# Four convolution and attention layers on one core: statistics gathered after 22 parts, weights and shifts of layer 0's end moved

## The chip, the cores and the metric

The kernel runs on 1 of the 8 cores of a Trainium2 chip. Its metric is the device time of one execution in microseconds (us), lower is better. Names used below: PE is TensorE (matrix products, with PEld its weight loads), DVE is VectorE, ACT is ScalarE, POOL is GpSimd, SP is SyncE, which mostly issues DMAs. Each engine works through its own list of instructions in order and waits for other engines through semaphores.

## The reference, cut to what matters

The input is x of 16 images, 256 channels, 28 x 28. Four layers follow each other.

```python
# layer 0
out = sign(x)                                   # binary activation, forward value
y = conv3x3(out, sign(weights)) * mean(|weights|)
x = (y - mean(y)) * rsqrt(var(y) + EPS) * gamma + beta + x      # mean, var over images and places
# layer 1
residual = prelu(x); z = sign(x + a_move)
y = prelu(bn(conv3x3(z, a_w)));  y = gate(.5*x + .5*y) * y * residual
y = bn(y) + residual;  u = prelu(bn(conv1x1(sign(y + f_move), f_w)))
x = bn(gate(.5*y + .5*u) * u) + y
# layer 2
out = prelu(conv3x3(sign(batchnorm(x)), sf1*sign(w1)))
out = prelu(conv3x3(sign(batchnorm(out)), sf2*sign(w2)))
x = prelu(batchnorm(out) + x)                   # batchnorm: statistics over images and places
# layer 3
q, k, v = Wq x, Wk x, Wv x
x = Wp (softmax(q k^T / 8) v) + x
```

Every batch norm needs the mean and the variance of a whole convolution's output before the next layer can read its first value. The convolutions of layers 0 and 2 therefore end in a point where everything waits for the last statistic.

## The kernel before

The 256 channels lie as two groups of 128 partitions. Layers 0 and 2 use the same function, `sign_layer`: a 3 x 3 convolution of signs by signs. Two groups of output channels are packed into one product (weights `a + 4095 b`), so one 128-wide product gives both, and they are taken apart afterwards. `sign_layer` walks through blocks. In layer 0 a block is a whole image (784 places), except that the last image is cut into a half and two quarters (`PARTS`, 33 parts in all; a whole image counts as two). In layer 2 a block is half an image (392 places, `HALVES`, 32 parts). For block j it emits, in this order:

1. `products(j)`: 18 products of PE for each half (6 packed weight chunks of 3 taps), into a PSUM tile `cv` of which there are three;
2. `sign_image`: on ACT, the signs of the next image, into one of two padded buffers `fpads`;
3. `post(j - 1)`: DVE's work on the block before. In layer 0 (`post0`) that is four or two BN_STATS over the block's values `n`, and a POOL-issued DMA of a finished image's int16 values to DRAM (`n0d`). In layer 2 (`post2`) it is a prelu into `p`, BN_STATS, twice, and on ACT a `square` of the sums, whose total is a guard against inexact results (`doubts`);
4. once, `moments.gather()`, at the first block whose part number is above `EARLY` (26): it merges the first 26 parts' statistics into three numbers, with one BN_AGGR per channel group and a scaling;
5. in layer 0, one entry of `steps`: pieces of weight work for later layers (load, ACT part, DVE part), dealt out one for each half image;
6. `apart(j)`: on ACT two passes that round the packed product (`t`, then `ab` or `n`), on DVE one that takes the other half (`ab` or `n`).

In this part the order on PE, ACT, DVE and SP is the program's own order (`manual_schedule`). POOL's order isn't; it is set by the framework's scheduler.

At the end of the convolution `Moments.__call__` merges the gathered numbers with the late parts' (a BN_AGGR over `fin`, 3 + 6 numbers for each late part), and `norm` or `sign_norm` works out scale and shift in a chain of tiny DVE instructions with one ACT square root. `keep_busy` gives PE dummy products (`unused`) for that time.

From layer 0 to layer 1: `norm("l0", ...)` gives the scale `r`, then calls `first`, which emits `enter(0, 0)` (image 0, channel group 0: scaled `n` plus x, one DVE instruction over two SBUF tensors). Then DVE works out `c = mean * r` and `bi0 = beta - c` in `norm`, and `zb1 = bi0 + a_move` behind it. `sign1(0, 0)` on ACT uses `zb1` as its bias; `transform` on DVE and `widen` make operands for PE's first product of layer 1. The values `n` are read back from `n0d` by SP DMAs, two buffers of which are there. Layer 1 is a loop over images (`iteration`), in which DVE and ACT prepare image b + 1 while PE works on image b.

The last two weight steps of layer 0 before the gates' weights are the sixth chunk of layer 2's first weights (`sign_weights`: ACT `sg`, DVE `wpk`) and the split of layer 1's 1 x 1 weights (`fw_step`, `split2`: DVE clips `stf`, ACT copies `fw`, DVE takes the remainder). Their loads are called by the steps two places earlier (`load_ahead`).

Of the kernel before, what the change touches and what calls it, by code (L numbers as in the profile page):

```python
# [51 lines left out]
IMAGES = [(i, 0, S) for i in range(B - 1)]  # L52
EARLY = 26
MC = 112
# [29 lines left out]
def forward(ctx: ExitStack, tc: tile.TileContext, d: dict, out: bass.AP, careful: bool):  # L84
# [16 lines left out]
    def pv(name):  # L101
        return vec[:, VECS.index(name), :]
# [27 lines left out]
    def vtile(name):  # L130
        return const.tile([P, 2], F32, name=name)

    def tt(o, a, b, op):
        V.tensor_tensor(o, a, b, op)  # L134
        return o
# [50 lines left out]

    def norm(name, moments, gamma, beta, sf=None, then=lambda r: None):


        half, e = vtile(name + "_half"), vtile(name + "_e")  # L190
        V.tensor_scalar(half, gamma, -0.5, None, ALU.mult)
        if sf is not None:

            tt(e, sf, sf, ALU.mult)
            V.tensor_scalar(e, e, 1e-30, 1.0 / EPS, ALU.max, ALU.mult)
            V.reciprocal(e, e)
        m, var = moments()
        v, c = vtile(name + "_v"), vtile(name + "_c")
        if sf is not None:
            tt(v, var, e, ALU.add)  # L200
        else:
            V.tensor_scalar(v, var, EPS, None, ALU.add)
        r = rsqrt(name, v, half)
        then(r)
        tt(c, m, r, ALU.mult)
        return r, tt(c, beta, c, ALU.subtract)

# [114 lines left out]
    def sign_layer(pads, w, temp, room, sign, post, steps, moments, blocks, together=1):  # L322
# [44 lines left out]
        with tc.manual_schedule(engines={ET.PE, ET.Activation, ET.DVE, ET.SP}):  # L367
            sign_image(0)
            for j, block in enumerate(blocks):
# [4 lines left out]
                if block[1] == 0 and block[0] + 1 < B:  # L374
                    sign_image(block[0] + 1)
                if j > 0:
                    post(blocks[j - 1], abs_[j - 1])
                if first_part(block) > EARLY and not gathered:
                    gathered = True
                    moments.gather()  # L380
                for p in range(len(pieces(block))):
# [3 lines left out]
                    late = step() if step else None  # L385
                apart(j)
            post(blocks[-1], abs_[-1])
        assert not steps and not late
# [31 lines left out]
    with tc.tile_pool(name="ps_conv", bufs=3, space=PSUM) as psc, \  # L420
# [13 lines left out]
        with tc.tile_pool(name="ph1", bufs=1) as ph:  # L434
# [109 lines left out]
            for t in (w_1, w_2):  # L544
                nc.gpsimd.memset(t, 0.0)

            def constants():
                for p in pads:
                    nc.gpsimd.memset(p, 0.0)
# [43 lines left out]
            for (_, high, low), taps, add_up, sign in zip(w1_steps, ahead[0::3], ahead[1::3], ahead[2::3]):  # L593
                steps += [taps, lambda high=high, low=low: (high(), low)[1], add_up, sign]
            steps += [ahead[-1], gate_weights]
            for i in (21, 17, 13, 9):
                steps[i:i] = [None]

            def post0(block, ab):
                b, r0, rows = block  # L600
                for mo in range(2):
                    for h, _, m in pieces(block):
                        V.bn_stats(mom.part(first_part(block) + h, mo), ab[:, mo, h * HN:h * HN + m * S])
                if r0 + rows == S:
                    nc.gpsimd.dma_start(out=n0d[b], in_=ns[b])

            mom = block_moments("l0", PARTS)
# [268 lines left out]
            def iteration(b):  # L876
# [67 lines left out]
                if two:  # L944
                    branch2(b - 2, 1, g[:, 1])
                    for k in range(2):
                        squares2(b - 2, k)
                lates = [s.work() for s in aside[b][::-1]]
                for s in aside[b + 1]:
                    s.load()  # L950
# [27 lines left out]

            with tc.manual_schedule(engines={ET.PE, ET.DVE, ET.Activation}):
                sc0, bi0 = norm("l0", mom, pv("g0"), pv("b0"), sf0, first)  # L980
                mom.doubt(doubts[:, 0:2 * NB])
                zb1 = tt(vtile("zb1"), bi0, pv("a_move"), ALU.add)
                sign1(0, 0)
# [95 lines left out]
        with tc.tile_pool(name="ph2", bufs=1) as ph:  # L1079
# [36 lines left out]
            def post2(order, alpha, mom, doubt):  # L1116
# [4 lines left out]
                def post(block, ab):  # L1121
# [18 lines left out]

                    for h, _, m in pieces(block) if not careful else ():

                        if i < B - 1:
                            square(h, m)
                        else:
                            last_squares.append(lambda h=h, m=m: square(h, m))
                return post
# [621 lines left out]
```

## Time and profile before

| | us |
|---|---|
| median of 3 runs | 970.87 (970.1 to 971.01) |
| the profiled execution | 969.59 |
| its span, first to last instruction | 967.7 |
| layer 0, from the start to PE's last product | 0 to 107.5 |
| between layers 0 and 1 (to PE's first product) | 107.5 to 117.7 |
| layer 1 and its end | 117.7 to 473.1 |
| layer 2, first convolution, then the gap | 473.1 to 571.2, to 579.1 |
| layer 2, second convolution, then the gap | 579.1 to 677.2, to about 690 |
| layer 3 | to 967.7 |

In the profile's timeline each line is a start, a duration, the engine, the line of the kernel, the operation, output <- inputs with their shapes, and in brackets how long the engine had stood idle and what ended that. `x2` after a shape means two instructions merged into one line. The granted clock is the share of TensorE's full clock that the throttle let through. `keep_busy` products count as busy PE time though they compute nothing, so PE's busy share between the layers says nothing of useful work.

### The profile page before, as it was taken

The page shows a single profiled execution, that of the slowest core. Times are in us where ns is not written, and L with a number is a line of the kernel's source. Part 1 is how long each engine was busy: PE and PEld are TensorE (multiplying, and loading weights), DVE is VectorE, ACT ScalarE, POOL GpSimd, SP SyncE. Part 2 cuts the span into 40 slices and gives each one's busy share as a digit, 9 for nine tenths or more (in the row PEclk, how much of TensorE's full clock was granted, in tenths as well). Part 3 has the DMA queues.
Part 4 walks back from the last instruction along what each step waited for, and adds up shares of the span by engine and source line. Part 5 has one row for each costly group of instructions (what it writes and reads, how often), then busy time and mean ns, then how long its engine had stood idle before and what let it go on. Part 6 is the DMA issues. An engine that isn't in the chain of part 4 may idle for free.

```text
span 967.7 us, 14795 instructions
## 1 busy us (share of the span) xinstructions
PE 942.3 (97%) x5609; PEld 582.1 (60%) x5615; DVE 773.8 (80%) x1418; ACT 721.7 (75%) x1198; POOL 140.9 (15%) x149
## 2 busy tenths in 40 slices
PE   7999899999999999999999999999999999999995
PEld 3555478788788778876555555555444444444442
DVE  4776878899998899976799987999756867777765
ACT  6887667888888888864888868887666667676652
POOL 3001100000000000000100000000145343444431
PEclk9999999999999999999999999999999999999999
DMA  9978512344433233100680000000043343435212
GB/s 348 343 267 304 177 34 84 116 149 146 145 125 100 100 113 111 60 34 34 232 334 1 1 1 1 2 1 1 5 76 88 80 122 72 129 71 131 67 67 104
DMA packets 26948, 105.82 MB, mean 109 GB/s; under 512 B 3490, under 2 KB 7268, under 8 KB 26868
## 3 DMA queue, kind: packets, MB, share of 16 engines
q1 hardware_dynamic: 20948, 73.44, 21.4%
q0 software_dynamic: 5632, 30.54, 11.7%
q8 instruction: 46, 0.75, 0.3%
q10 hardware_dynamic: 288, 0.80, 0.2%
q14 instruction: 34, 0.28, 0.1%
HBM read 72.67 MB, written 32.11 MB: 108 GB/s over the span
## 4 chain that ended last, share of the span: by engine, by line
PE 46%; DVE 3%; ACT 1%; issue 1%; DVEq 0%; ACTq 0%
PE cv L340 19%; PE sc L1344 8%; PE av L1365 8%; PE mi L1321 4%; PE sm L1407 2%; PE mi L1425 2%; PE sm L1365 1%; DVE p L1131 1%; DVE ab L354 0%; ACT es L1348 0%; DVE l2b_fin L1133 0%; DVE l2c_fin L1133 0%; DVE r L1391 0%; DVE p L1308 0%; DVE p L1307 0%
## 5 line engine op out<-in xcount | busy, mean ns | idle before, releaser
L340 PE MATMUL cv<-fpads,wpk 128*128 128x392 f16 (+1 forms) x1746 | 294.7, 331 | 4.3 <-DVE wpk L267 2.3
L718 PE MATMUL cv<-vs,w 128*128 128x392 bf16 (+1 forms) x1536 | 286.9, 356 | 4.1 <-DVE vs L134 4.1
L340 PEld LDWEIGHTS <-wpk 128*128 128x128 f16 x1746 | 169.0, 97 | 130.4 <-DVE wpk L267 3.7
L718 PEld LDWEIGHTS cv<-vs,w 128*128 128x128 f32 x768 | 142.5, 190 | 11.0 <-ACT vs L700 0.2
L1348 ACT ACTIVATE es<-sc 128x784 f32<-128x784 f32 x112 | 87.3, 822 | 41.1 <-PE sc L1344 41.1
L718 PEld LDWEIGHTS <-w 128*128 128x128 f16 x768 | 67.9, 101 | 59.6 <-issue 18.7
L1344 PE MATMUL sc<-q,keyswa 64*128 64x392 f32 x448 | 89.9, 513 | 0.9 <-ACT es L1348 0.9
L1131 DVE SCALAR_TENSOR_TENSOR p<-ab,vec 128x392 f32<-128x392 f32 x128 | 79.1, 618 | 2.3
L1365 PE MATMUL av<-es,v 128*64 128x392 f32 x448 | 80.7, 499 | 0.0
L1358 POOL TENSOR_TENSOR sum<-sum,es 128x784 f32<-128x784 f32 x32 | 67.2, 2099 | 3.1 <-ACT es L1348 0.6
L1344 PEld LDWEIGHTS sc<-q,keyswa 64*128 64x128 f32 x448 | 38.9, 186 | 44.0 <-issue 17.1
L351 ACT ACTIVATE t<-cv,rounding 128x392 f32<-128x392 f32 (+2 forms) x82 | 51.8, 632 | 13.3 <-PE cv L340 10.4
L861 POOL DMA_DIRECT2D x2d<-x x16 | 8.6, 537 | 343.4 <-DVE x L855 280.9
L1332 DVE COPY keyswa<-mi 64x392 f32<-64x392 f32 x31 | 16.3, 565 | 52.6 <-ACT q L1328 52.6
L1365 PEld LDWEIGHTS av<-es,v 128*64 128x64 f32 x448 | 29.4, 136 | 47.4 <-issue 47.0
L700 ACT CAST vs<-vs 128x840 fp32r<-128x840 bf16 x63 | 54.1, 882 | 2.2 <-DVE vs L134 2.2
L1136 ACT ACTIVATE t<-ab 128x392 f32<-128x392 f32 x64 | 33.5, 524 | 27.9 <-DVE ab L354 27.9
L833 PE MATMUL cv<-z,fw 128*128 128x392 f32 x256 | 48.9, 342 | 1.0 <-ACT z L825 0.8
L354 DVE SCALAR_TENSOR_TENSOR ab<-ab,cv 128x392 f32<-128x392 f32 x64 | 35.5, 555 | 17.5 <-ACT ab L352 17.5
L833 PEld LDWEIGHTS cv<-z,fw 128*128 128x128 f32 x256 | 45.7, 188 | 2.3 <-ACT z L825 2.1
L1321 PE MATMUL mi<-p,wqk 128*128 128x392 f32 x124 | 45.3, 506 | 0.3 <-DVE p L1308 0.3
L1356 POOL TENSOR_TENSOR sum<-es 128x784 f32<-128x784 f32 x16 | 30.0, 1877 | 91.0 <-ACT es L1348 91.0
(288 smaller groups left out, 1519.8 us busy)
## 6 DMA issues: line engine op xcount, KB each, us to landing
xs<-in_x_dram SPq DMA_DIRECT2D x30, 784.0 KB, 5.5
x2d<-x POOLq DMA_DIRECT2D x16, 784.0 KB, 3.8
out_dram<-p SPq DMA_DIRECT2D x15, 784.0 KB, 3.9
p<-x2d POOLq DMA_DIRECT2D x14, 784.0 KB, 6.9
p<-x2d SPq DMA_DIRECT2D x13, 784.0 KB, 15.6
n0d<-n POOLq DMA_DIRECT2D x16, 392.0 KB, 5.1
n<-n0d SPq DMA_DIRECT2D x16, 392.0 KB, 3.1
st<-in_w_dram SPq DMA_DIRECT2D x12, 384.0 KB, 6.7
```

The source lines that it names most:

```text
L340: T.matmul(pss[j][:, n // size if careful else h, :rows * S].rearrange("p (a b) -> p a b", b=S), lhsT=w[:, n, t, :], rhs=pads[:, blocks[j] ...
L351: A.activation(by_halves(t, blocks[j]), ps, AF.Identity, bias=rounding, scale=1.0 / PACK)
L354: V.scalar_tensor_tensor(a, b, -PACK, ps, ALU.mult, ALU.add)
L700: copy(v, w)
L718: T.matmul(ps.rearrange("p (a b) -> p a b", b=S), lhsT=w[:, k, c, u, mo * P:(mo + 1) * P], rhs=v[:, b % 2, u, k, :, c:c + S], start=((part ...
L833: T.matmul(ps[:, h, :HN], lhsT=w[:, k, mo * P:(mo + 1) * P], rhs=z2[b][:, k, h * HN:(h + 1) * HN], start=(k + i == 0), stop=(k + i == 2),)
L1131: V.scalar_tensor_tensor(p, y, alpha[:, mo:mo + 1], y, ALU.mult, ALU.max)
L1321: T.matmul(ps[:, h, :HN], lhsT=wqk[:, k, :], rhs=x[b][:, k, h * HN:(h + 1) * HN], start=(k == 0), stop=(k == 1))
L1344: T.matmul(ps[:, h, :HN], lhsT=chunk[rows], rhs=qs[b][rows], start=True, stop=True)
L1348: A.activation(e, ps[:, :, :HN], AF.Exp, scale=0.125)
L1358: (V if late else nc.gpsimd).tensor_tensor(sums[b, late], sums[b, late], e, ALU.add)
L1365: T.matmul(ps[64 * h:64 * h + 64, :HN], lhsT=w, rhs=e[:, h, :], start=start, stop=stop)
```

## The change

Four things change.

- `EARLY` is 22 and not 26: in all three convolutions of `sign_layer` the gather merges 22 parts and comes four parts earlier, and four more parts stay for the final BN_AGGR.
- In layer 2 `post` returns its squares instead of emitting them, and `sign_layer` emits them after `apart(j)`. On ACT the order goes from signs, square, t, ab to signs, t, ab, square. The last image's squares are still emitted after the convolution.
- The last two weight steps are taken out of layer 0's list (two empty places stand for them) and are emitted in iteration 0 of layer 1, behind the second channel group's sums and `widen`.
- In layer 0's norm `c`, `zb1` and `bi0` are computed on POOL, `zb1` from a sum `moved = b0 + a_move` that DVE makes early in layer 0. `enter(0, 1)` now follows `enter(0, 0)` on DVE at once.

```diff
-EARLY = 26
+EARLY = 22
...
-    def norm(name, moments, gamma, beta, sf=None, then=lambda r: None):
+    def norm(name, moments, gamma, beta, sf=None, then=lambda r: None, shifts=()):
...
         then(r)
-        tt(c, m, r, ALU.mult)
-        return r, tt(c, beta, c, ALU.subtract)
+        if not shifts:
+            tt(c, m, r, ALU.mult)
+            return r, tt(c, beta, c, ALU.subtract)
+        cs = [vtile(f"{name}_c{i}") for i in range(len(shifts))]
+        nc.gpsimd.tensor_tensor(c, m, r, ALU.mult)
+        for o, b in zip(cs, shifts):
+            nc.gpsimd.tensor_tensor(o, b, c, ALU.subtract)
+        return r, *cs
...
-                if j > 0:
-                    post(blocks[j - 1], abs_[j - 1])
+                after = post(blocks[j - 1], abs_[j - 1]) if j > 0 else ()
...
                 apart(j)
+                for f in after:
+                    f()
...
             def constants():
+                tt(moved, pv("b0"), pv("a_move"), ALU.add)
...
-            steps += [ahead[-1], gate_weights]
+            last_weights = [steps.pop(), ahead[-1]]
+            steps += [None, None, gate_weights]
...
                 lates = [s.work() for s in aside[b][::-1]]
+                if b == 0:
+                    lates += [late for late in [w() for w in last_weights] if late]
...
-                sc0, bi0 = norm("l0", mom, pv("g0"), pv("b0"), sf0, first)
+                sc0, zb1, bi0 = norm("l0", mom, pv("g0"), pv("b0"), sf0, first, (moved, pv("b0")))
                 mom.doubt(doubts[:, 0:2 * NB])
-                zb1 = tt(vtile("zb1"), bi0, pv("a_move"), ALU.add)
...
-                    for h, _, m in pieces(block) if not careful else ():
-
-                        if i < B - 1:
-                            square(h, m)
-                        else:
-                            last_squares.append(lambda h=h, m=m: square(h, m))
+                    squares = [lambda h=h, m=m: square(h, m) for h, _, m in pieces(block) if not careful]
+                    if i < B - 1:
+                        return squares
+                    last_squares.extend(squares)
+                    return ()
```

## The prediction

> **What bounds the kernel now.** I read the page's busy shares first, then busy time by stage, then the timeline where TensorE (PE) stops. Busy shares, then stages (stretch, length, busy PE, weight loads, DVE, ACT, POOL, granted clock, DMA share, GB/s):
>
> ```profile
> PE 942.3 (97%) x5609; PEld 582.1 (60%) x5615; DVE 773.8 (80%) x1418; ACT 721.7 (75%) x1198; POOL 140.9 (15%) x149
> 107.50:117.70 10.20, 6.28 (x32) 2.78 (x31) 8.94 (x31) 3.81 (x8) 1.47 (x5) 1.00 0.38 121
> 117.70:470.00 352.30, 349.75 (x1981) 276.35 (x1984) 303.33 (x648) 281.78 (x426) 8.47 (x18) 1.00 0.29 96
> 571.20:579.10 7.90, 6.44 (x30) 2.86 (x30) 6.67 (x20) 3.35 (x9) 0.84 (x1) 1.00 0.00 0
> ```
>
> PE is the bound inside the stages: 349.75 of 352.30 us in layer 1. Between stages its busy time is dummy products of `keep_busy`; there a chain through DVE sets the end. So an edit gains only if it shortens such a chain, and whatever moves it moves all that follows. Timeline between layers 0 and 1 (start, us, engine, line, what):
>
> ```profile
> 107.53 1.04 DVE L603 BATCH_NORM_STATS2 l_fin<-n 128x6 f32<-128x392 int16 x2
> 108.49 0.54 DVE L267 SCALAR_TENSOR_TENSOR wpk<-sg 128x384 f16<-128x384 bf16 x1
> 108.94 0.42 DVE L302 TENSOR_SCALAR stf<-stf 128x512 f32<-128x512 f32 x1
> 110.05 0.69 DVE L134 TENSOR_TENSOR fw<-stf,fw 128x512 fp32r<-128x512 f32 x1 [0.41 <-ACT fw L303]
> 110.86 0.36 DVE L354 SCALAR_TENSOR_TENSOR n<-n,cv 128x196 int16<-128x196 int16 x1
> 112.72 0.56 DVE L184 BATCH_NORM_AGGREGATE l_mv<-l_fin 128x2 f32<-128x45 f32 x2
> 114.67 1.04 DVE L674 SCALAR_TENSOR_TENSOR xs<-n,l_r,xs 128x784 f32<-128x784 int16 x1
> 116.27 1.86 ACT L680 ACTIVATE pad<-xs,zb 128x784 bf16<-128x784 f32 x2 [2.49 <-DVE zb L134]
> 117.69 0.68 PE L718 MATMUL cv<-vs,w 128*128 128x392 bf16 x3 [3.87 <-DVE vs L134]
> ```
>
> The products end at 107.5 and the dummies at 113.82. DVE spends 108.49 to 110.86 on weights while two quarter images wait. After PE's 3.87 us of rest the clock is halved, 118.62 to 122.02 by the finest clock windows (columns: stretch, length, PE, clock, DMA, GB/s):
>
> ```profile
> 118.75:119.00 0.25, 0.25 (x2) 0.50 0.78 301
> ```
>
> The end of layer 2's first convolution; the second is the same, 105.96 us later:
>
> ```profile
> 560.54 1.56 DVE L167 BATCH_NORM_AGGREGATE l2b_fin<-l2b_parts 128x2 f32<-128x156 f32 x2
> 562.22 0.56 DVE L354 SCALAR_TENSOR_TENSOR ab<-ab,cv 128x392 f32<-128x392 f32 x1
> 573.67 0.55 DVE L354 SCALAR_TENSOR_TENSOR ab<-ab,cv 128x392 f32<-128x392 f32 x1
> 579.08 2.15 PE L340 MATMUL cv<-fpads,wpk 128*128 128x392 f16 x11 [1.43 <-ACT fpads L1097]
> ```
>
> `gather` holds DVE from 560.54 to 562.22. The four blocks after it come 2.8625 us apart with DVE never idle, and PE has been through since 571.2: DVE is late to the end.
>
> **The change, part by part.**
>
> **Gather after 22 parts, layer 2.** An aggregate takes 0.821 us for 156 numbers and 0.328 for 39, 4.2 ns a number; so 132 take 0.72, and the gather 1.68 - 0.20 = 1.48. It stands ahead of block 23 in place of 27. In the old pattern block 23 starts on DVE at 548.31 and DVE stands idle 0.3 us once an image. With 1.48 of lateness and eight steps of 2.8625, block 31 starts at 548.31 + 1.48 + 22.90 = 572.69, not 573.67: 0.98 gained (PE's own end plus 1.22 of ACT would allow 572.45). The final aggregates grow by 24 numbers, 0.10 each, two in a row: -0.20. Net 0.78 per convolution. Behind the first the dummies end at 577.65, before the new start at 578.30: all of it counts. Behind the second they end at 686.85 and real work starts at 687.15; four fp32 pairs of 0.93 then end at 690.57, where the chain had 691.30 (690.37 + 0.93): capped at 0.73. Together **1.5**; if lateness isn't worked off, -0.40.
>
> **Squares behind the next reads.** In the steady state ACT issues the same set per image (t, ab, two signs, squares), so nothing. After the gather ACT waits 1.1 us for DVE's ab before each square, but its own chain back to DVE is 2.38 a block against DVE's 2.86: still nothing. Signs of the next image now come one square (0.7) later; they finished 556.0 for a need at 558.98. Taken at 0; without that cover 0.7 a layer.
>
> **Weights moved to layer 1.** Off the tail: wpk, stf, fw and the waits, 110.86 - 108.49 = 2.37. ACT's t and n of the first quarter image (0.42, 0.46, PE done by 106.2) are then ready by 107.2, those of the second by 108.5, before DVE wants them. Two tiny instructions for e now stand between, 0.10 taken (0 to 0.2). The bigger aggregates cost 0.20. So r and `enter(0, 0)` come 2.07 earlier, at 112.60. The layer 0 gather falls where DVE idles 1.5 us an image (row ahead of 92.18): 0. The sum for `moved`, 0.16, hides there too.
> What is late next is the re-read of n0d for image 0: issued at 108.97, unchanged, since it waits for image 14's write; such reads land in 2.9 to 4.2, at 111.9 to 113.2, and now image 15's write runs beside it. 0 taken, up to 0.6 in the range.
> The loads keep their places on SP: they are called by steps two places earlier, which stay.
> In iteration 0 they add on ACT 0.83 + 0.62 and on DVE 0.42 + 0.69 + 0.54 plus 0.7 of waiting for ACT's fw behind sg: 2.35. Queued behind on DVE: transforms for image 1 (needed over 4 us later), `rows_out`, `enter(2, ...)`, the sums for the hidden product of iteration 1. Cover: DVE idles 0.27 + 1.46 there, and the sums are ready at 141.95 for a product at 143.88, 1.93; 3.66 in all. So 0 unless PE itself runs ahead.
>
> **Shifts on POOL.** Before, sign 0 starts 1.60 after `enter(0, 0)` (116.27 - 114.67). Without c, beta and zb on DVE it could start 1.12 after (as 124.61 to 125.73 in iteration 0): gain 0.48 if POOL's three 0.22 us instructions (its 128x14 row; its queue is clear: image 15's write and four doubts end about 111.9) run beside `enter`. I doubt that, from attention:
>
> ```profile
> 744.27 1.85 POOL L1356 TENSOR_TENSOR sum<-es 128x784 f32<-128x784 f32 x1 [5.60 <-ACT es L1348]
> 744.92 2.02 DVE L1358 TENSOR_TENSOR sum<-sum,es 128x784 f32<-128x784 f32 x1
> 746.19 4.39 POOL L1358 TENSOR_TENSOR sum<-sum,es 128x784 f32<-128x784 f32 x2
> ```
>
> Alone DVE's takes 0.96 (L1361) and POOL's 1.85; overlapped, DVE's takes 2.02, ending 0.8 after POOL's, and POOL's next takes 2.46. They shut each other out, and POOL resumes 0.15 before DVE's end. `enter` reads two SBUF tensors as well. DVE starts it 0.04 after r, POOL reacts about 0.15 after (94.37 behind a statistic). So POOL's c waits to 0.89 after `enter(0, 0)` starts, `enter(0, 1)` then shuts zb1 out to about 2.0 (or goes first, and both follow): sign 0 starts 2.3 to 2.45 after, not 1.60. That costs 0.78 in place of gaining 0.48. I take the cost: it is the nearer row. Shift of PE's start: 2.07 - 0.78 = **1.3** (2.55 without the shutting out).
> The Trainium skill ("SBUF — State Buffer", the rules on the shared port pair) says that any VectorE instruction with two SBUF inputs and a GpSimd one that reads SBUF exclude each other for whole instructions; by it the 0.78 is due, and the sum without it would be 1.3 us better. The rows show this for TENSOR_TENSOR only.
>
> **The clock.** The halved stretch is 3.40 us long and costs 1.6 us of layer 1, whose PE is the bound. The two gaps of 1.43 and below show none. The new gap, 117.69 - 1.3 - 113.82 = 2.6, lies between. The stretch began one such length after 115.21, and between these PE rested 2.7 us; the length before held 1.4 us of rest and was followed by no halving at 117.7 to 118.5. Cut at the same instants, 2.6 falls into 1.4 and 1.2: no halving. I take **1.6**, bounds 0 and 1.6. PE then runs 1.6 ahead of DVE: 2.35 + 1.6 - 3.66 = **-0.3**.
> The Trainium skill ("TensorE: Matmul & The Clock Gate", the HAM clock gate) wants a whole idle window of some 3.4 us, free-running: by it 2.6 never halves the clock. The trace is stricter: 2.7 us of rest sufficed.
>
> **Sum.** 1.3 + 1.6 - 0.3 + 1.5 = 4.1. Span 967.7 - 4.1 = 963.6; this execution took 969.59 (1.89 around its span), and the median, 970.87, stands 1.28 above: 966.8.
>
> **The rivals.** *POOL is not shut out* (0.22): 2.55 + 1.6 - 0.3 + 1.5 = 5.35, 965.5. For: no row overlaps POOL with this instruction; against: the rows above.
> *The clock is still halved* (0.25): 1.3 + 1.5 = 2.8, 968.1. For: 2.6 is near 2.7, and where the cuts fall may differ from run to run.
> *The early gather isn't worked off* (0.07): 1.3 + 1.6 - 0.3 - 0.4 = 2.2, 968.7. Against: 0.3 of idle per image.
> *POOL holds layer 1 up, slower* (0.06): with d for each of c and zb1, sign 0 starts at 112.7 + 2d; against 116.27 and with 1.5 back, no change is at d = 2.5, and d = 4 gives 970.87 + 4.4 - 1.5 = 973.8. For: at 4.72 tiny DVE instructions took 3.04 us while POOL's memset ran. Against: nothing longer than 1.04 is here to shut POOL out.
>
> **How the numbers follow.** The forecast has 0.40. About 0.2% (1.9 us) is what a measurement of this kernel tells from no change. Range 965.0 to 969.0: from no shutting out to late gather, with 0.6 for the re-read; it leaves out the slower case and the outer parts of the others. Faster 0.88 (the three first cases and part of the fourth), same 0.06, slower 0.06.
>
> **What would show it.** Block 31 of each layer 2 convolution about 1.0 earlier behind PE's end; no weights between 108 and 111; aggregates of about 0.42; c and zb1 on POOL stretched and sign 0 2.3 after `enter(0, 0)` (1.1 if not shut out); PE's rest near 2.6 with clock 1.00; a wait of 0.3 ahead of iteration 1's hidden product. Wrong if layer 1's PE waits in iterations 0 to 2, or if n0d's re-read is what `enter` waits for.

## The result, and the profile after

The changed kernel took 964.97 us (median, 964.09 to 965.61), the kernel before 969.97 beside it (968.51 to 971.01): a ratio of 0.9949, 95% interval 0.9936 to 0.9962. It is faster by 0.5%, as forecast; the time lies 1.8 below the predicted 966.8 and 0.03 below the range. The profiled execution took 964.49 with a span of 962.7, 5.0 shorter than the span before.

The page gives the busy shares of the changed kernel. Below them stands its busy time by the same three stretches as before (stretch, length, busy PE, weight loads, DVE, ACT, POOL, granted clock, DMA share, GB/s):

```profile
PE 942.6 (98%) x5615; PEld 582.4 (60%) x5615; DVE 772.7 (80%) x1416; ACT 718.7 (75%) x1198; POOL 143.0 (15%) x152
```

```profile
107.30:115.60 8.30, 6.21 (x30) 2.65 (x28) 6.79 (x24) 2.48 (x5) 3.60 (x8) 1.00 0.50 156
115.60:466.40 350.80, 348.41 (x1983) 275.49 (x1984) 304.52 (x651) 283.03 (x428) 8.47 (x18) 1.00 0.28 96
567.40:574.65 7.25, 6.61 (x32) 2.88 (x31) 6.10 (x18) 2.83 (x7) 0.84 (x1) 1.00 0.00 0
```

The stretch between layers 0 and 1 is 8.3 long instead of 10.2, layer 1 is 1.5 shorter, and the stretch inside layer 2 is 0.65 shorter (0.78 counted between real products, as below). This is the timeline of the first of them (start, us, engine, line, what, idle time before it):

```profile
110.02 0.77 DVE L184 BATCH_NORM_AGGREGATE l_mv<-l_fin 128x2 f32<-128x69 f32 x2
112.12 1.03 DVE L686 SCALAR_TENSOR_TENSOR xs<-n,l_r,xs 128x784 f32<-128x784 int16 x1
112.17 1.04 POOL L209 TENSOR_TENSOR l_c<-l_mv,l_r 128x2 f32<-128x2 f32 x1 [0.64 <-DVE l_r L148]
113.29 0.88 POOL L211 TENSOR_TENSOR l_c<-moved,l_c 128x2 f32<-128x2 f32 x1
114.13 0.19 POOL L211 TENSOR_TENSOR l_c<-vec,l_c 128x2 f32<-128x2 f32 x1
114.20 1.79 ACT L692 ACTIVATE pad<-xs,l_c 128x784 bf16<-128x784 f32 x2 [2.97 <-POOL l_c L211]
115.62 0.68 PE L730 MATMUL cv<-vs,w 128*128 128x392 bf16 x3 [2.11 <-DVE vs L134]
```

No weight step stands ahead of the aggregates any more. Of the same GpSimd instruction on two numbers, the free one took 0.19 and those beside `enter` 1.04 and 0.88; sign 0 starts 2.08 after `enter(0, 0)`. The timeline of layer 2's first convolution shows the gather, the first and the last `ab` behind it, and the first product of the second convolution:

```profile
544.67 1.34 DVE L167 BATCH_NORM_AGGREGATE l2b_fin<-l2b_parts 128x2 f32<-128x132 f32 x2
546.13 0.56 DVE L360 SCALAR_TENSOR_TENSOR ab<-ab,cv 128x392 f32<-128x392 f32 x1
569.02 0.55 DVE L360 SCALAR_TENSOR_TENSOR ab<-ab,cv 128x392 f32<-128x392 f32 x1
574.65 98.05 PE L346 MATMUL cv<-fpads,wpk 128*128 128x392 f16 x576 [0.64 <-ACT fpads L1110]
```

Counted from the convolution's first product (473.13 before, 469.48 after), the last block's `ab` starts 99.54 after it, not 100.54.

The next table shows where the 5.0 us come from, by the same TensorE products in both timelines. Layer 0's end is the end of its last product, 107.77 before; at the 107.5 of the table ahead of the prediction TensorE begins to load the dummies' weights. The flag is one number made from the guards at the very end, for which the last products wait.

| product | before | after | difference | gained in this step |
|---|---|---|---|---|
| last of layer 0 (its end) | 107.77 | 107.46 | -0.31 | 0.31 |
| first of layer 1 | 117.69 | 115.62 | -2.07 | 1.76 |
| hidden product of `mix_c` | 128.34 | 124.61 | -3.73 | 1.66 |
| gate product of iteration 1 | 146.42 | 142.85 | -3.57 | -0.16 |
| first of layer 2 | 473.13 | 469.48 | -3.65 | 0.08 |
| first of its second convolution | 579.08 | 574.65 | -4.43 | 0.78 |
| last pair of `keys_to` ahead of attention | 690.37 | 685.13 | -5.24 | 0.81 |
| last values, ahead of the flag | 953.54 | 948.27 | -5.27 | 0.03 |

Behind the flag the changed kernel gives 0.68 back (VectorE's last sum starts at 955.94, not 960.53) and wins 0.4 while the last store lands. The loss is a clock halved at the very end, which the kernel before did not show there; the column before the DMA share is the granted clock:

```profile
950.40:953.80 3.40, 1.22 (x12) 0.47 (x8) 2.73 (x8) 0.94 (x3) 0.00 (x0) 1.00 0.00 2
953.80:955.70 1.90, 1.90 (x16) 1.76 (x12) 0.87 (x3) 0.00 (x0) 0.00 (x0) 0.51 0.06 17
```

### The profile page after: what moved, and what is told of

Read it like the earlier page. It is cut to its first block, busy times and chain, and to the rows that moved or that the text cites. A ratio compares the mean times of both kernels' runs of the same rounds, so it can differ in the third digit from the quotient of the medians.

```text
span 962.7 us, 14797 instructions
## 1 busy us (share of the span) xinstructions
PE 942.6 (98%) x5615; PEld 582.4 (60%) x5615; DVE 772.7 (80%) x1416; ACT 718.7 (75%) x1198; POOL 143.0 (15%) x152
## 4 chain that ended last, share of the span: by engine, by line
PE 41%; DVE 7%; ACT 2%; issue 1%; DVEq 0%; ACTq 0%
PE cv L346 14%; PE sc L1356 8%; PE av L1377 8%; PE mi L1333 4%; DVE p L1144 2%; PE sm L1419 2%; PE mi L1437 2%; PE sm L1377 1%; DVE ab L360 1%; DVE l2c_fin L1146 1%; DVE l2b_fin L1146 1%; ACT fpads L1110 1%; ACT es L1360 0%; DVE r L1403 0%; DVE p L1320 0%
## 5 line engine op out<-in xcount | busy, mean ns | idle before, releaser
L439 PE MATMUL unused<-idle 128*128 128x512 bf16 x175 | 41.2, 393 | 3.0 <-POOL idle L475 3.0
```

## The experiments

Effects here are 0.3 to 2 us and executions of one kernel spread over 0.5 to 4, so each verdict rests on distances in the timeline first (say, from layer 0's last product to layer 1's first: 9.92 before, 8.16 after) and on the median second. Medians are given against the kernel before, measured beside them; the changed kernel stood at -5.0. In brackets stands the ratio with its 95% interval. The kernel before had medians of 968.72 to 969.97 in these measurements, so a difference of under 1 between two of them rests on the timelines alone.

### Layer 2: when the gather comes, and where the squares stand

```diff
-EARLY = 22
+EARLY = 26
```

> The changed kernel with EARLY = 26 again, all else as changed. Theory (the gather's 1.5 us is worked off over eight blocks when it comes early and over four when late): each convolution of layer 2 ends its tail 0.8 later (TensorE's end of products to next real product), 1.57 us in the two; layer 0's two aggregates shrink from 0.77 to 0.56, so TensorE starts layer 1 0.2 earlier. In sum 1.2 to 1.5 longer than the changed kernel, -3.6 against the kernel before. Rival (VectorE is saturated from the gather to the end, so it matters not when it comes, and the smaller final aggregates win): 0.6 us shorter than the changed kernel, -5.6.

Measured: 967.34, -1.8 (0.9978, 0.9966 to 0.9990).

```diff
                 after = post(blocks[j - 1], abs_[j - 1]) if j > 0 else ()
+                for f in after:
+                    f()
+                after = ()
```

> The changed kernel with the squares of layer 2 issued ahead of the next block's reads again, as in the kernel before. Theory (ScalarE is not what the tail waits for): ScalarE waits for ab ahead of its squares again, some 28 us in the two convolutions, and nothing moves: each tail of layer 2, from the last product of the convolution to the next real product, stays within 0.1 of the changed kernel's, and the time within 0.2. Rival (behind the gather the reads come late because the square waits for ab, so VectorE does not work its lateness off): the last block's ab is 0.4 to 0.7 later behind the last product than the changed kernel's 1.65, and the time 0.8 to 1.4 longer.

Measured: 965.48, -4.0 (0.9952, 0.9935 to 0.9970). With the two kernels these two runs give all four combinations of the two edits. The table has the time of the first convolution, from its first product to the first product of the second, and in brackets that of the second, up to the last pair of `keys_to`:

| | squares ahead of the reads | squares behind them |
|---|---|---|
| gather after 26 parts | before: 105.95 (111.29) | 105.97 (111.29) |
| gather after 22 parts | 105.50 (110.81) | after: 105.17 (110.48) |

The early gather is worth 0.80 in each convolution behind moved squares, as the theory had it (1.61 in the two), and 0.45 to 0.48 without them. The squares are worth nothing beside the late gather and 0.33 beside the early one: both the zero of the theory and the rival's 0.4 to 0.7 miss that. The next two views are of the kernel with the squares back: ScalarE's waits (waiter, releaser, us in total, times, longest), and VectorE's blocks after the gather:

```profile
ACT t L1152 <- DVE ab L360: 27.4, 38, 1.1
```

```profile
550.59 0.55 DVE L360 SCALAR_TENSOR_TENSOR ab<-ab,cv 128x392 f32<-128x392 f32 x1
553.45 0.54 DVE L360 SCALAR_TENSOR_TENSOR ab<-ab,cv 128x392 f32<-128x392 f32 x1
556.47 0.56 DVE L360 SCALAR_TENSOR_TENSOR ab<-ab,cv 128x392 f32<-128x392 f32 x1
559.34 0.54 DVE L360 SCALAR_TENSOR_TENSOR ab<-ab,cv 128x392 f32<-128x392 f32 x1
562.35 0.56 DVE L360 SCALAR_TENSOR_TENSOR ab<-ab,cv 128x392 f32<-128x392 f32 x1
```

The steps are 2.86, 3.02, 2.87, 3.01. This is ScalarE's own timeline in the last of them:

```profile
558.72 1.96 ACT L1113 ACTIVATE fpads<-p,l2a_c,vec 128x784 f16<-128x784 f32 x2
560.58 0.51 ACT L1152 ACTIVATE t<-ab 128x392 f32<-128x392 f32 x1
561.09 0.57 ACT L357 ACTIVATE t<-cv,rounding 128x392 f32<-128x392 f32 x1
561.69 0.62 ACT L358 ACTIVATE ab<-t,unrounding 128x392 f32<-128x392 f32 x1
```

First come the two signs of the next image, then the square, and only then the reads, which end at 562.31; VectorE's `ab` starts at 562.35, right behind them. The long steps, 0.31 in all, are the two with signs; in the changed kernel all eight steps are 2.85 to 2.88. So the last 0.33 of the catching up needs ScalarE's new order. In the kernel before, the last signs of this convolution run from 560.14 to 562.10, beside the late gather itself, and no later block has any; there the order costs nothing.

The first kernel's -1.8 in place of -3.6 is not layer 2's. Of its ten executions five list a mean granted clock of 0.994 and took 967.48 to 969.30, and five list 0.997 or 0.998 and took 965.23 to 967.21. The profiled one, of the first group, has the clock halved in layer 1 after a rest of TensorE of only 1.98. Columns: stretch, length, PE, clock, DMA share, GB/s:

```profile
114.00:117.40 3.40, 1.48 (x8) 1.00 0.69 222
117.40:120.80 3.40, 3.40 (x13) 0.50 0.01 2
```

From the first product of layer 1 to the hidden product of `mix_c` it takes 10.51, not 8.99. The kernel with the squares back, whose rest is 2.11 to the hundredth like the changed kernel's, is halved too (10.57):

```profile
113.50:117.00 3.50, 1.24 (x7) 1.00 0.78 213
117.00:120.40 3.40, 3.40 (x12) 0.50 0.04 17
```

### The moved weights, and the clock alone

```diff
-            last_weights = [steps.pop(), ahead[-1]]
-            steps += [None, None, gate_weights]
+            last_weights = []
+            steps += [ahead[-1], gate_weights]
```

> The changed kernel with the last two weight steps (sg and wpk, stf and fw) back in layer 0's last blocks. Theory (they stand on VectorE between the last quarter images, and the longer rest of TensorE halves its clock): wpk, stf and fw stand between 108 and 111 again, enter(0, 0) comes 2.3 to 2.5 later, the first product of layer 1 as much, TensorE rests 4.5 us ahead of it instead of 2.1, the clock is halved for 3.4 us, which costs another 1.6, and the wait ahead of iteration 1's hidden product (0.25) is gone. In sum 3.8 to 4.0 longer than the changed kernel, about -1.1 against the kernel before. Rival 1 (the weights hide behind the re-read of n0d, which enter waits for): 0.5 longer at most, -4.5. Rival 2 (the clock does not depend on that rest): 2.3 longer, -2.7, the first products of layer 1 at 0.23 us.

Measured: 968.06, -1.06 (0.9989, 0.9979 to 0.9999), as the theory had it. The first product of layer 1 in its timeline:

```profile
118.74 11.44 PE L730 MATMUL cv<-vs,w 128*128 128x392 bf16 x48 [4.53 <-DVE vs L134]
```

It comes 10.57 after layer 0's last product, 2.41 more than in the changed kernel, and the clock is halved from 117.6 to 124.4, two lengths of 3.4 instead of one.

```diff
-            keep_busy(28)
+            keep_busy(44)
```

This edit is made in the kernel before, behind layer 0.

> The kernel before with 44 dummy products in place of 28 behind layer 0: they end at 113.82 + 16 x 0.221 = 117.36, 0.3 us ahead of the first product of layer 1, which the chain through VectorE sets at 117.69. Nothing else is changed, so this is the clock alone. Theory (TensorE's rest of 3.87 us is what halves the clock afterwards): no halved stretch between 118 and 122, iteration 0 is 1.6 us shorter, a wait of about 0.2 stands ahead of a later product, and the time is 1.3 to 1.6 shorter than the kernel before. Rival (the halved stretch comes of what starts there, products on fresh weights beside the casts, not of the rest): the stretch stays and the time is that of the kernel before.

Measured: 967.61, -1.5 (0.9985, 0.9975 to 0.9995). Its timeline:

```profile
107.74 9.44 PE L432 MATMUL unused<-idle 128*128 128x512 bf16 x43
117.60 0.68 PE L718 MATMUL cv<-vs,w 128*128 128x392 bf16 x3 [0.41 <-DVE vs L134]
```

Sixteen dummy products are the only edit. The clock stays at 1.00, and `mix_c`'s product comes 9.06 after the first instead of 10.65: the rest was the cause, and its price is 1.6.

### The shifts

```diff
-        nc.gpsimd.tensor_tensor(c, m, r, ALU.mult)
+        tt(c, m, r, ALU.mult)
         for o, b in zip(cs, shifts):
-            nc.gpsimd.tensor_tensor(o, b, c, ALU.subtract)
+            tt(o, b, c, ALU.subtract)
```

> The changed kernel with c, zb1 and bi0 of layer 0's norm on VectorE, behind the first enter, zb1 straight from moved. Theory (GpSimd is shut out while enter runs): in the changed kernel GpSimd's c took 1.04 us and zb1 0.88, and sign 0 started 2.08 us after enter(0, 0). On VectorE c and zb1 follow the first enter (0.96) at 0.19 each, so sign 0 starts 1.40 after it, 0.68 earlier, TensorE's first product of layer 1 as much, and the end 0.5 to 0.7 earlier than the changed kernel's (about -5.6 us against the kernel before, where the changed kernel had -5.0). Rival (three instructions off VectorE's queue are a gain, for VectorE is what iteration 1's hidden product waits for): the 0.58 us that VectorE gets back shows up as a longer wait there, 0.25 becoming 0.8, and the time stays at that of the changed kernel or is up to 0.5 longer.

Measured: 964.59, -4.5 (0.9950, 0.9932 to 0.9968). Its timeline:

```profile
113.61 1.04 DVE L686 SCALAR_TENSOR_TENSOR xs<-n,l_r,xs 128x784 f32<-128x784 int16 x1
115.01 1.93 ACT L692 ACTIVATE pad<-xs,l_c 128x784 bf16<-128x784 f32 x2 [2.28 <-DVE l_c L134]
116.43 0.68 PE L730 MATMUL cv<-vs,w 128*128 128x392 bf16 x3 [1.43 <-DVE vs L134]
```

Sign 0 comes 1.40 after `enter(0, 0)`, and layer 1 starts 7.47 after layer 0's last product, 0.69 sooner than with GpSimd: the theory's 0.68. The wait that the rival saw growing, ahead of iteration 1's hidden product, is 0.30, not 0.8. The median does not show the gain. In this profile the clock was also halved from 10.3 to 13.7, in layer 0's first image, and layer 0 ended 1.5 later than in the changed kernel's; the edit does not touch layer 0.

```diff
+        if shifts:
+            minus = vtile(name + "_minus")
+            V.tensor_scalar(minus, m, -1.0, None, ALU.mult)
         r = rsqrt(name, v, half)
         then(r)
...
+        for k in range(2):
+            A.activation(
+                cs[0][:, k:k + 1], r[:, k:k + 1], AF.Identity, bias=shifts[0][:, k:k + 1], scale=minus[:, k:k + 1]
+            )
         nc.gpsimd.tensor_tensor(c, m, r, ALU.mult)
-        for o, b in zip(cs, shifts):
-            nc.gpsimd.tensor_tensor(o, b, c, ALU.subtract)
+        nc.gpsimd.tensor_tensor(cs[1], shifts[1], c, ALU.subtract)
```

> The changed kernel with zb1 made on ScalarE straight from r (two 128x1 instructions, r times minus the mean plus moved; the minus is taken on VectorE while it waits for the root), bi0 stays on GpSimd. Theory (shut-out GpSimd costs, and sign 0 can start once the first enter has written): zb1 is ready 0.5 after r, sign 0 starts 1.0 to 1.1 after enter(0, 0) where the changed kernel's starts 2.08 after and the VectorE form's 1.4, TensorE's first product comes 1.0 earlier than the changed kernel's, counted from the last product of layer 0 (8.16 there, so 7.1 to 7.2), and the end 0.8 to 1.0 earlier. Rival (ScalarE's two instructions and the wait for r stretch as GpSimd's did, for ScalarE reads the same memory): sign 0 at 2.0 or later, no gain. Second rival (VectorE in iteration 0 is the bound): the first product comes 1.0 earlier, but the wait ahead of iteration 1's hidden product grows from 0.25 to over 1, and the end stays.

Measured: 963.77, -5.7 (0.9943, 0.9927 to 0.9958). Its timeline:

```profile
112.16 0.66 ACT L213 ACTIVATE l_c<-l_r,moved,l_minus 128x1 f32<-128x1 f32 x2 [0.89 <-DVE l_r L148]
112.16 1.03 DVE L692 SCALAR_TENSOR_TENSOR xs<-n,l_r,xs 128x784 f32<-128x784 int16 x1
113.37 1.83 ACT L698 ACTIVATE pad<-xs,l_c 128x784 bf16<-128x784 f32 x2 [0.55 <-POOL l_c L216]
114.79 0.68 PE L736 MATMUL cv<-vs,w 128*128 128x392 bf16 x3 [1.24 <-DVE vs L134]
```

ScalarE is not held up beside `enter`: its two instructions take 0.66 together. Sign 0 comes 1.21 after `enter`, and `mix_c`'s product at 123.82 instead of 124.61. The wait ahead of iteration 1's hidden product is 0.29, not over 1, so both rivals fall.

### What is late next: rests, the re-read, and the order of two instructions

```diff
-            keep_busy(28)
+            keep_busy(36)
```

> The changed kernel with 36 dummy products behind layer 0 in place of 28: TensorE rests 0.3 us ahead of layer 1 instead of 2.11. Nothing else moves, so this asks whether the changed kernel's rest still halves the clock in some of its executions. Theory (windows of 3.41 us whose cuts stand anywhere in the program: the kernel with the shifts on VectorE had halved stretches from 10.36 and from 955.76, 277 windows apart; the window ahead of a halved stretch held 1.8 to 3.4 us of rest, windows with 1.7 or less were not followed by one, by the runs so far): 2.11 + 0.15 of rest lie for more than 1.75 in one window in (3.41 + 2.26 - 3.5) / 3.41 = 0.64 of the executions, where iteration 0 costs 1.5 more. Without the rest the mean time falls by some 0.6 x 1.5 = 0.9, median 0.5 to 1.2 shorter than the changed kernel, -5.5 to -6.2 against the kernel before, and the profile shows no halved stretch between 112 and 125. Rival (a rest below some fixed length near 2.1 to 3.8 never halves the clock, the halved stretch of the kernel with EARLY = 26 after a rest of 1.98 being something else): the same time as the changed kernel, -5.0 against the kernel before.

Measured: 964.74, -4.75 (0.9952, 0.9938 to 0.9965), 963.73 to 965.55. No halved stretch stands ahead of 954 in the profile, but the expected gain of the median is not there. The five executions list mean clocks of 0.994 to 0.997, the two longest 0.994; where the halved lengths of the unprofiled ones lay is not recorded. Two things in the timeline were new:

```profile
112.55 0.20 POOL L209 TENSOR_TENSOR l_c<-l_mv,l_r 128x2 f32<-128x2 f32 x1 [0.63 <-DVE l_r L148]
112.82 0.20 POOL L211 TENSOR_TENSOR l_c<-moved,l_c 128x2 f32<-128x2 f32 x1
112.83 1.03 DVE L686 SCALAR_TENSOR_TENSOR xs<-n,l_r,xs 128x784 f32<-128x784 int16 x1 [0.36 <-DMA n<-n0d]
113.95 1.86 ACT L692 ACTIVATE pad<-xs,l_c 128x784 bf16<-128x784 f32 x2 [2.35 <-POOL l_c L211]
```

`enter` waited 0.36 for the re-read of image 0, and while it waited GpSimd's c and zb1 got through in 0.20 each. Sign 0 then came 1.12 after `enter`, and layer 1 started 7.60 after layer 0's last product, 0.56 sooner than in the changed kernel, in spite of the wait.

The next kernel puts together what the runs so far pointed to:

```diff
-EARLY = 22
+EARLY = 20
...
-    def block_moments(name, blocks):
-        return Moments(name, EARLY, len(blocks) - EARLY, EARLY * HN)
+    def block_moments(name, blocks, early=EARLY):
+        return Moments(name, early, len(blocks) - early, early * HN)
...
-            keep_busy(10)
+            keep_busy(12)
...
-            mom = block_moments("l0", PARTS)
+            mom = block_moments("l0", PARTS, 26)
...
-            keep_busy(28)
+            keep_busy(32)
...
-            keep_busy(45)
+            keep_busy(43)
...
+        keep_busy(7)
         up = raise_flag(two_banks(psmi, "mi")[:, 0, :])
+        keep_busy(2)
```

To these come zb1 on ScalarE, as above, and `sign_layer` gathers after the parts of its own moments.

> Everything that the runs so far point to, in one kernel: the changed kernel with zb1 on ScalarE, layer 0's statistics gathered after 26 parts and layer 2's after 20, dummy products to fill TensorE's rests (32 behind layer 0, 12 in place of 10 at the start, 7 and 2 around the flag at the end) and 43 instead of 45 behind layer 2. Theory: sign 0 1.0 earlier; layer 0's aggregates 0.15 shorter; each tail of layer 2 another 0.3 shorter (two more blocks to work off VectorE's lateness at 0.19 each, less 0.1 for larger final aggregates); the halved clock at the end, which cost the changed kernel's profile 0.65, gone; none at 10 or at 117. In sum 2.4 shorter than the changed kernel's profile, 3 in the median, about -7.5 to -8 against the kernel before. Rival (the terms overlap: a TensorE that starts layer 1 earlier waits for VectorE in iteration 0 instead, and GpSimd and SyncE bring the re-reads late): 1.0 to 1.5 shorter than the changed kernel, -6 to -6.5.

Measured: 964.40, -5.1 (0.9942, 0.9928 to 0.9956), 963.20 to 966.06. Its timeline:

```profile
112.17 0.19 POOL L216 TENSOR_TENSOR l_c<-l_mv,l_r 128x2 f32<-128x2 f32 x1 [0.54 <-DVE l_r L148]
113.92 1.03 DVE L692 SCALAR_TENSOR_TENSOR xs<-n,l_r,xs 128x784 f32<-128x784 int16 x1 [1.83 <-DMA n<-n0d]
116.55 5.72 PE L736 MATMUL cv<-vs,w 128*128 128x392 bf16 x21 [2.02 <-DVE vs L134]
```

The re-read of n0d for image 0 waits for image 14's write, since it takes that image's buffer; here it was issued at 109.93 (108.22 in the changed kernel's profile), took 3.78 to land (2.96 there), and `enter` stood 1.83 for it. TensorE then rested 2.02 and was halved from 117.1. With `enter` late, GpSimd's c took 0.19 again. Each tail of layer 2 was 0.05 to 0.06 shorter than the changed kernel's, not 0.3: VectorE was no longer late (it waited 0.3 for a product once). The next kernel adds one edit to this one:

```diff
-                    ns[b] = ph.tile([P, 2, N], I16, tag="n", name=f"n{b}", bufs=2)
+                    ns[b] = ph.tile([P, 2, N], I16, tag="n" if b else "rn", name=f"n{b}", bufs=2)
                     nc.sync.dma_start(out=ns[b], in_=n0d[b])
```

> The kernel with everything together, and one more edit: the re-read of n0d for image 0 goes to a buffer that layer 0 leaves unused (tag rn) instead of image 14's, so it no longer waits for image 14's write. Theory (what the kernel with everything together lost was that re-read: enter(0, 0) was ready at 112.09 and waited 1.83 for it, TensorE then rested 2.02 and its clock was halved from 117.06): the re-read is issued some 2 us earlier and has landed by 111.5; enter(0, 0) starts at 112.1, sign 0 at 113.3, TensorE's first product at 114.7 without a rest of over 0.4, no halved stretch between 10 and 955. Profile 3.3 shorter than that of the kernel before this edit, span about 961; median about 961 to 962, -8 against the kernel before, and fewer long executions. Rival 1 (the re-read lands late because the DMA queues are full with image 15's write and layer 1's loads, not because it is issued late): the wait ahead of enter(0, 0) stays, 0.4 to 1.8, and the time with it. Rival 2 (a TensorE that starts 1 us earlier waits for VectorE in iteration 0): first product at 114.7, but a wait of over 0.8 ahead of the hidden product of iteration 1, median 962.5 to 963.

Measured: 963.33, -5.9 (0.9941, 0.9928 to 0.9955), 963.03 to 963.76. Its timeline:

```profile
112.45 1.05 DVE L692 SCALAR_TENSOR_TENSOR xs<-n,l_r,xs 128x784 f32<-128x784 int16 x1
115.10 0.68 PE L736 MATMUL cv<-vs,w 128*128 128x392 bf16 x3 [0.26 <-DVE vs L134]
```

The wait for the re-read is gone, layer 1 starts after a rest of 0.26, and no stretch from 10 to 955 is halved. The span, 961.5, came out near the expected 961, though this layer 0 ended 0.31 later, at 107.93. The median missed the expected 961 to 962, because the time of an execution is some 1.8 longer than its span (963.33 for 961.5 here), and the expectation set the two nearly equal.

The same edit alone, on the changed kernel:

> The changed kernel with that one edit alone: the re-read of n0d for image 0 in a buffer of its own. In the profiled execution of the changed kernel enter(0, 0) did not wait for the re-read; in one kernel of the same layer 0 it waited 0.36, in another 1.83. Theory (the moved weights have made this re-read the next limit, in some executions only): the profile's start of layer 1 is as in the changed kernel, 8.1 to 8.2 after layer 0's last product; the longest executions become rarer, and the median falls by 0.2 to 0.6, -5.2 to -5.6 against the kernel before. Rival (those waits came of the other edits in those kernels): the same time as the changed kernel, -5.0.

Measured: 963.69, -5.5 (0.9945, 0.9932 to 0.9959). But its profile starts layer 1 7.24 after layer 0's last product, not 8.1 to 8.2, for a reason that neither theory had:

```profile
112.16 1.05 DVE L686 SCALAR_TENSOR_TENSOR xs<-n,l_r,xs 128x784 f32<-128x784 int16 x1
112.18 0.20 POOL L209 TENSOR_TENSOR l_c<-l_mv,l_r 128x2 f32<-128x2 f32 x1 [0.64 <-DVE l_r L148]
112.46 0.80 POOL L211 TENSOR_TENSOR l_c<-moved,l_c 128x2 f32<-128x2 f32 x1
113.30 1.86 ACT L692 ACTIVATE pad<-xs,l_c 128x784 bf16<-128x784 f32 x2 [2.05 <-POOL l_c L211]
```

GpSimd's c started 0.02 behind `enter` and got through in 0.20; zb1 then waited `enter` out, and sign 0 came 1.14 after it. In the changed kernel c started 0.05 behind and was held for 1.04.

This order goes with the edit. Counted from the start of the instruction that ends r, c starts 0.25 later in all of these profiles. `enter` starts 0.20 later in the six that have c on GpSimd, the old buffer and no wait for the re-read, and there c is held for 1.04; it starts 0.22 later in the three with a buffer of its own, and there c takes 0.20. Why `enter` starts 0.02 later with its own buffer is not shown. Since neither profile of the unedited changed kernel waits for the re-read, the 0.92 by which layer 1 starts sooner here is this order; what the edit saves in executions with a late re-read can't be told from this run.

The profiled execution is nevertheless the longest of its five, 965.15: its clock is halved at the flag, and its span ends 7.80 after VectorE's last sum begins, 6.7 to 7.2 in all other profiles.

Last, the changed kernel and the kernel with everything, unedited, on one chip:

> The changed kernel itself, unedited, on one chip with the kernel of the next run. Theory (its time hangs on three accidents in an execution: where the clock's windows of 3.41 us fall on TensorE's rest of 2.1, worth 1.6; whether GpSimd's c starts before or after enter(0, 0), worth 0.9; whether the re-read of n0d has landed, worth 0 to 1.8): the profile shows another combination of the three than the first one, and the times spread over 1.5 to 3 us, median 964.5 to 965.5, -4.4 to -5.2 against the kernel before. Rival (the changed kernel always runs as its profile did): spread under 1 us, -5.0.

> The kernel with everything together and the re-read in a room of its own, unedited, beside the changed kernel on one chip. Theory (it has taken the three accidents out): times within 1 us of one another again (0.73 in its first run), median 963.0 to 963.6, 1.0 to 2.0 shorter than the changed kernel's on the same chip, no halved stretch between 15 and 950. Rival (its lower median was the chip's): within 0.5 of the changed kernel's.

Measured: the changed kernel 964.59, -4.1 (0.9952, 0.9939 to 0.9966), 962.80 to 965.25, a spread of 2.45; the other 963.45, -5.3 (0.9942, 0.9928 to 0.9955), 963.13 to 963.64, a spread of 0.51. Over both measurements the medians are 964.59 (eleven executions) and 963.39 (ten). The version with everything beats both kernels, by 1.2 over the changed one. Both of its profiles start layer 1 7.2 after layer 0's last product, not 8.2 as both of the changed kernel's do. Some of what it takes out is chance: the changed kernel's best execution, 962.80, is ahead of all of its own. The changed kernel's second profile shows, against the theory, the same combination as its first (c held for 1.04, rest 2.11, no halving in layer 1). So the spread of its times is shown, but not what made each time. The clock has a part in it: in this second measurement the shortest execution lists a mean clock of 0.998 and the longest 0.994. It is not all, for in the first measurement the longest, 965.61, lists 0.996, more than the shortest.

## Why the prediction was right, and where it was not

**Sum.** Forecast 4.1, measured 5.0 in the span. That is 0.9 of the 1.8 by which the time was missed; another 0.8 is the step from the profiled execution to the median, 1.28 before and 0.48 after. The kernel before itself stands at 969.97 with three more executions, 0.9 below the 970.87 from which the forecast counted.

**Gather.** Right in mechanism and size: block 31's `ab` 1.00 earlier (forecast 0.98), the two aggregates 0.21 longer (0.20), 0.78 and 0.81 per convolution (0.78 and 0.73). Lateness was worked off, but with the squares in their old place only 0.45 and 0.48 of the gain would have come.

**Squares.** This is the step that failed: "its own chain back to DVE is 2.38 a block against DVE's 2.86: still nothing". That chain left out ScalarE's two signs per image, which the next sentence treated only as a possible delay for TensorE. With them, two of the eight blocks after the gather take 3.02 and 3.01, and the forecast's 1.5 would have been 0.93 (0.45 + 0.48). That the forecast of the whole came out here is luck: the change happened to have both edits, and the prediction gave the squares no part in the gain.

**Weights.** Right: `enter(0, 0)` came 2.24 earlier, counted from layer 0's end (forecast 2.07); putting them back cost 2.41. They cost nothing in iteration 0 beyond the wait that the sum had as -0.3; the timeline shows it at the hidden product of iteration 1, 0.25 long, and the products lose 0.16 there:

```profile
140.21 0.52 PEld L640 LDWEIGHTS hid<-g,se 128*128 128x128 f32 x4 [0.25 <-DVE g L134]
```

**Re-read.** Taken at 0 with up to 0.6. In the changed kernel's profiles it was 0, in two later kernels 0.36 and 1.83: what is late next was named rightly, but for those kernels its upper bound was too small, in one by three times. It was worked out from how long such reads take, not from how late they may be issued.

**Shifts.** The shutting out was right: c and zb1 took 1.04 and 0.88. The term was mis-sized: the forecast had zb1 shut out "to about 2.0", with its own time and ScalarE's start still to come; measured, zb1 was done 2.05 after `enter(0, 0)` began, and sign 0 followed 0.03 behind it, at 2.08, not at 2.3 to 2.45. So the price was 0.48, not 0.78, and layer 1 started 1.76 earlier, not 1.3. The rows with the shifts on VectorE (1.40) and ScalarE (1.21) confirm the sign: this part of the change costs 0.7 against the plainest alternative. The 1.12 that the forecast gave for the case without shutting out is also seen, where c was not held: 1.12 with 36 dummies and 1.14 with the buffer of its own. The Trainium skill ("SBUF — State Buffer", the rules on the shared port pair) says that whichever of two such instructions starts first has the pair to itself until it ends. The rows agree that one is held for the whole of the other, and now for this instruction with an int16 and an f32 input. On which goes first they agree only up to 0.02 us of the recorded starts: c took 0.20 when its start stood 0.02 behind that of `enter`, and 1.04 at 0.05.

**Clock.** Measured 1.66 for a forecast 1.6, and no halving after the rest, as forecast; but the argument for it, "Cut at the same instants, 2.6 falls into 1.4 and 1.2", assumed cuts that stand still in the program. They do not (last section): with the changed kernel's own rest of 2.11 (forecast 2.6), one of three profiles was halved. By that section a rest of 2.11 with 0.15 behind it escapes only if a cut leaves less than 1.83 on each side, in some 1.4 of 3.41 us, so as an estimate it is halved in 0.6 of the executions. That the profiled one kept its clock was luck, and 0.25 was a low chance for the rival "the clock is still halved".

**What no step had.** Two things had no term in the sum: the halved clock at the end (-0.68), and layer 0's end, 0.31 earlier, which is chance, for in the runs here it lies between 107.5 and 109.0.

## What to carry to other kernels

Before calling an edit worth nothing beside saturated engines, add up each engine's whole set of instructions per image, those for the next image too; an engine that is late only gains from work moved earlier if every other engine can follow its pace. Tiny instructions on GpSimd behind a VectorE instruction with two SBUF inputs were held until that one ended (0.8 to 1.04 us in place of 0.20); here ScalarE, which was waiting anyway, did them without being held up. When a change brings a chain's end down to that of a transfer or to a rest near 1.8 us, the time of single executions becomes a matter of chance, and it is worth taking the chance out (another buffer, a few dummy products) before measuring anything finer.

## What the runs showed of the hardware

Halved stretches are 3.4 us long or a multiple of it, except where the program's end cuts them off, and their beginnings lie on a grid: in the kernel with the shifts on VectorE they began at 10.28 and at 955.76, 945.48 apart, which is 277 lengths of 3.413. Where the grid stands in the program differs from execution to execution. What decides is TensorE's rest within one length ahead. In order of that rest, worked out from the products' starts and ends:

| kernel | grid length | rest in it, us | clock after it |
|---|---|---|---|
| changed | 114.17 to 117.58 | 1.60 | 1.00 |
| before, at the flag | 954.89 to 958.31 | 1.78 | 1.00 |
| shifts on VectorE, start | 6.87 to 10.28 | 1.84 | 0.50 |
| EARLY = 26 | 113.98 to 117.39 | 1.93 | 0.50 |
| everything together | 113.65 to 117.06 | 2.02 | 0.50 |
| changed, at the flag | 950.43 to 953.84 | 2.18 | 0.50 |
| squares back | 113.55 to 116.96 | 2.25 | 0.50 |
| before | 115.23 to 118.64 | 2.68 | 0.50 |

Over all fourteen profiles, from where their record of the clock begins (6 to 9 us), no length at full clock with 1.82 us of rest or less was followed by a halved one, and each with 1.84 or more was. So about half a length of rest, 1.8 of 3.41 us, in one piece or several, halves the next length, and a rest shorter than 3.4 is halved or not by where the grid cuts it. Once halved, less is needed to stay so: with the weights back, 117.6 to 121.0 held 1.15 of rest and the clock stayed down for another length. The Trainium skill ("TensorE: Matmul & The Clock Gate", the HAM clock gate) has free-running windows of 3413 ns, and the trace agrees with that; it asks for a window of idleness, and there the trace differs: 1.84 us were enough.
